# Attention and mixture of experts in one launch: weight loads a head ahead, packed probabilities, a ring of single rows for the gathers

## The chip, the cores and the metric

One core of a Trainium2 chip runs the whole program in one launch. The metric is the time of one execution on the device in microseconds (us), and the median of several executions is compared. Engines are named as in the profile: PE is TensorE, PEld its weight loads, DVE VectorE, ACT ScalarE, POOL GpSimd, SP SyncE. Line numbers (L83) are those of the kernel before.

## The reference, cut to what matters

```python
# B, S, D = 4, 512, 512;  H, HD = 16, 128;  E, K, I, SI = 16, 6, 352, 704
x = x + xattn(layernorm(x), ctx)             # softmax((ctx Wq' + bq)(ctx Wk' + bk)'), one head
hid = layernorm(x)
h = rmsnorm(hid, ln1_w)
q, k, v = h @ wq, h @ wk, h @ wv             # 16 heads of 128
scores = where(causal, q k' / sqrt(HD), -1e9)
hid = hid + (softmax(scores) v) @ wo
t = rmsnorm(hid, ln2_w)
probs = softmax(t @ gate_w.T); topv, topi = top_k(probs, 6); topv /= sum(topv)
routed = sum over the 6 chosen e: topv_e * ((silu(t eg_e') * (t eu_e')) @ ed_e')
shared = (silu(t sg') * (t su')) @ sd'
out = x + hid + routed + shared
```

Everything is float32. The kernel holds each float32 operand as a pair of float16 values (high part and remainder), and each product of the reference is three matmuls: high times high, high times remainder, remainder times high (`mm3`, L83, L86 and L87).

## The kernel before, in words

**Stages.** `xattn(b)` (a generator, one `yield` per piece) makes the first attention and the transposed input `hT[b]` of the second for each of four batches. Then comes a loop over 64 heads, which takes two batches at a time so that two neighbouring groups use the same weights (`path`, `heads`; a group `g` is two heads of one batch). After the heads come the shared feed-forward (`gate_up`, `shared_down`) of batches 0, 1 and 2, then 16 experts in order of their load, and the shared feed-forward of batch 3 as the last.

**One turn of the head loop (turn n).** `queries` computes the head's queries and keys (24 matmuls of 128x512, tiles `qk`, split into `qkt` by one ACT and one DVE instruction each). Every second turn `values` makes the values of both heads of the group. Then `project` (the output projection `wo` of a group that is complete), `scores(n)`, and `attend(n - LAG)` with LAG = 1. `scores` makes four blocks of rows (widths 128, 256, 384 and 512, since the mask is causal); each goes from PSUM through DVE (mask and maximum, L671), ACT (exp, L673), DVE (reciprocal, L675 and L676), ACT and DVE (`split` into float16 pairs, L73 and L74) into `pn`, and is then turned by a DMA transpose on SP's queue (`flip`, L91) into the tile `pt`. `attend` (tile `av`) multiplies `pt` by the values and splits the result into `ao`. So a head's `av` matmuls wait for the last of four transposes.

`pt` has 2 x 4 rows of 512: the transposed probabilities of key block k stand at rows 2k and 2k+1, and half of the rectangle is never written. `attend` runs over k, with one product of width 512, 384, 256 and 128 each: 4 x 3 = 12 matmuls and 3 x 1280 columns for each head.

**Weights.** The first use of each weight loads float32 into a staging tile, splits it, and writes the float16 pair to DRAM (L423, L429). The second pair of batches loads that pair (`fetch`, L414). All of these are DMAs on POOL's queue, issued in the turn that uses them, as far as the scheduler does not hoist them. The pools of `wqk`, `wv` and `wo` have two buffers each.

**Routing.** When a batch's last group is projected, `route1`, `route2` and `route3` normalize it, compute its gates (`lg`), rank the tokens within each expert (`rk`) and put 24 scatters of rows into a list. `scatter` issues a few of them in each turn (indirect DMAs on POOL, L467), and `pace` puts a one-element copy (`mark`, L457) that reads a recent result in front of them, so that they do not run ahead. In `route2` a running sum over the 16 experts takes four steps, each a DVE copy (L580) and a POOL addition (L581).

**Closing turns.** For n = 64 and 65 the first six pieces of `gate_up(0)` are mixed in, three in each turn.

**Gathers.** From the eleventh expert on, the expert results of each token are gathered from DRAM, one rank at a time: 16 indirect DMAs for each rank (`gather`, L1169 on POOL), each followed by an addition on DVE (L1178), which is pinned in program order. Their tiles hold three rows of 512 (2 buffers, six places), and the addition is issued when more than four gathers are outstanding.

**Order.** The program is written in this order, and a scheduler then moves instructions on each engine by the costs that it assumes; each engine runs its own list strictly in order. `after(a, b)` fixes an order of two instructions on one queue.

Of the kernel before, what the change touches and what calls it, by code (L numbers as in the profile page):

```python
# [9 lines left out]
F16 = mybir.dt.float16  # L10
# [7 lines left out]
P = 128  # L18
# [23 lines left out]
ON = 60  # L42
ROWS = E * T + 1
# [6 lines left out]
LAG = 1  # L50
# [5 lines left out]
def xattn_moe_block_kernel(ctx: ExitStack, tc: tile.TileContext, x, xT, ctxT, wqkx, bqk, ln1, ln2,  # L56
# [112 lines left out]
    ht = bpool("ht")  # L169
# [34 lines left out]
    def xattn(b):  # L204
# [37 lines left out]
        def wide(nm):  # L242
            return (ap_ if b else ht).tile([P, 2 * C, S], F16, tag=nm if b else "pt", name=f"{nm}{b}")
# [161 lines left out]
    held, partner, seen = {}, {}, set()  # L405

    def fetch(b, g, pool, tag, n, src, scr, nm):
        if held.get(nm, (None,))[0] == (b, g):
            return held.pop(nm)[1]
        w = pool.tile([P, 2, n], F16, tag=tag, name=f"{nm}_{b}")  # L410
        if (b, g) in partner:
            held[nm] = partner[b, g], w
        if nm in seen:
            nc.gpsimd.dma_start(w.rearrange("p a n -> p (a n)"), scr)  # L414
            return w
# [4 lines left out]
        else:  # L420
# [3 lines left out]
            if nm == "wqk1":  # L424
                after(ins, zz["hT", 0])
        for j, ins in enumerate(split(w[:, 0], w[:, 1], st_[:, :n], WS)):
            if first:
                after(ins, zz["nb"] if j else zz["calm"][0])
        ins = (nc.sync if nm == "wqk0" else nc.gpsimd).dma_start(scr, w.rearrange("p a n -> p (a n)"))  # L429
        if nm != "wqk0":  # L430
            zz["pad"] = ins
        if nm == "wqk0":
            after(ins, zz["ptp", 0])
        return w

# [20 lines left out]
    def pace(src):  # L456
        ins = nc.gpsimd.tensor_copy(mark, src)  # L457
        if "rrs" in zz:
            after(ins, zz["rrs"])
# [72 lines left out]
    def route2(b):  # L532
# [45 lines left out]
        for sft in (1, 2, 4, 8):  # L578
            nx = rp.tile([P, NT, E], F32, name="rcs", bufs=2)
            nc.vector.tensor_copy(nx[:, :, :sft], cs[:, :, :sft])  # L580
            nc.gpsimd.tensor_tensor(nx[:, :, sft:], cs[:, :, sft:], cs[:, :, :E - sft], ALU.add)  # L581
# [41 lines left out]
    def values(b, g):  # L623
        hb = hT[b]
        wvt = fetch(b, g, wg, "wv", C * GW, wv[g], wv_d[g], f"wv{g}").rearrange("p a (c d) -> p a c d", c=C)
# [11 lines left out]
    def queries(b, h):  # L637
        hb = hT[b]
        wt = fetch(b, h // HG, wp, "wqk", 1024, wqk[h], wqk_d[h], f"wqk{h}").rearrange("p l (a c d) -> p l a c d", a=2, c=C)
# [14 lines left out]
    def scores(b, h):  # L654
        qk = qks[b, h]
        pt = pts[b, h] = ht.tile([P, 2 * NT, S], F16, tag="pt", name="pt")
        for t in range(NT):
# [22 lines left out]
            flip(pt[:, :2 * (t + 1), tl], pn)  # L680

    def attend(b, h):
# [7 lines left out]
        for k in range(NT):  # L690
            mm3(pv[:, k * P:], [(vt[:, k, 0, hl], vt[:, k, 1, hl], pt[:, 2 * k, k * P:],
                                 pt[:, 2 * k + 1, k * P:])], start=k == 0, stop=k == NT - 1)
        split(ao[:, hh, 0], ao[:, hh, 1], pv, 1.0 / PS)

    def project(b, g):
# [4 lines left out]
        wot = fetch(b, g, wg, "wo", HG * D, wo[g], wo_d[g], f"wo{g}").rearrange("p a (c d) -> p a c d", c=HG)  # L700
# [15 lines left out]
    def gate_up(b, hid, tmp):  # L716
# [577 lines left out]
```

## Time and profile before

| what | value |
|---|---|
| median of 3 runs | 1769.27 us (1768.77 to 1786.13) |
| the profiled execution's own time | 1762.41 us |
| its span, first to last instruction | 1760.7 us |
| PE busy | 1708.6 us (97%), 9919 matmuls |
| DVE, ACT, POOL busy | 1116.2, 829.3, 485.1 us |
| mean granted TensorE clock | 0.993 |

A matmul's busy time reaches into the next one, since they are pipelined; the distance from one start to the next is what a matmul costs. The list of waits gives for each engine and line the idle time in front of it and what ended it, as a total, a count and the longest. Five columns matter in a timeline: start, duration, engine, line, and in brackets the idle time before it with its releaser.

### The profile page before, as it was taken

Reading aid. Unit: us, or ns where it says so; the run is one execution under the profiler, and the core shown is the slowest. Engines: PE = TensorE matmul, PEld = TensorE weight load, DVE = VectorE, ACT = ScalarE, POOL = GpSimd, SP = SyncE. Lnnn points to the kernel's source line nnn. Section 1 sums busy time; section 2 is a strip of 40 time slices with the busy share of each in tenths; the row PEclk is TensorE's granted clock in tenths of the full one; section 3 lists DMA queues with packets and bytes.
Section 4 is the critical chain, followed back from the end, with each engine's and each line's share of the span. In section 5 each row is a group of like instructions: output and inputs, shape, how many; then the busy total and the mean of one; then the engine's idle time right before and its main releaser. Section 6 shows DMA issues by size and latency. Waiting matters only on the chain. (4 is left out here: it accounts for less than half of the span.)

```text
span 1760.7 us, 27659 instructions
## 1 busy us (share of the span) xinstructions
PE 1708.6 (97%) x9919; PEld 932.9 (53%) x9919; DVE 1116.2 (63%) x2766; ACT 829.3 (47%) x1711; POOL 485.1 (28%) x614
## 2 busy tenths in 40 slices
PE   7899999999998999999999999999999999999998
PEld 3555556565654555556555544455555555555553
DVE  6787877787785676776667647544434344356755
ACT  4565655565643545454445422344544445444431
POOL 5524212240255242121113454300000000034654
PEclk9999999999999999999999999999999999999999
DMA  7787867575687787556547653755554546589866
GB/s 246 181 205 184 225 150 192 122 196 118 138 183 187 163 177 179 120 120 118 111 104 132 140 155 128 247 173 148 150 173 137 154 143 163 154 228 254 221 198 213
DMA packets 392212, 296.24 MB, mean 168 GB/s; under 512 B 334880, under 2 KB 335136, under 8 KB 391296
## 3 DMA queue, kind: packets, MB, share of 16 engines
q1 hardware_dynamic: 353360, 159.87, 39.9%
q0 software_dynamic: 38704, 134.51, 25.5%
q8 instruction: 80, 1.31, 0.3%
q14 instruction: 68, 0.56, 0.1%
HBM read 124.81 MB, written 88.94 MB: 121 GB/s over the span
## 5 line engine op out<-in xcount | busy, mean ns | idle before, releaser
L1169 POOL DMA_INDIRECT yg<-y_d,yrc x96 | 109.9, 1145 | 505.2 <-PE u L87 426.0
L673 ACT ACTIVATE pe<-pe,bnm 128x128 f32<-128x128 f32 (+3 forms) x256 | 142.5, 557 | 161.5 <-DVE bnm L671 161.3
L83 PE MATMUL qk<-hT,wqk 128*128 128x512 f16 (+1 forms) x520 | 196.4, 378 | 9.1 <-DMA wqk<-wqk_d 5.5
L86 PE MATMUL qk<-hT,wqk 128*128 128x512 f16 (+1 forms) x520 | 196.5, 378 | 0.0
L87 PE MATMUL qk<-hT,wqk 128*128 128x512 f16 (+1 forms) x520 | 196.3, 377 | 0.0
L74 DVE SCALAR_TENSOR_TENSOR pn<-pe,brc,pn 128x128 f16<-128x128 f32 (+3 forms) x256 | 148.1, 590 | 21.3 <-ACT pn L73 18.0
L671 DVE CUSTOM_DVE_ANT_0 pe<-sc,causal 128x128 f32<-128x128 f32 (+3 forms) x256 | 117.0, 485 | 66.9 <-PE sc L668 65.9
L73 ACT ACTIVATE pn<-pe,brc 128x128 f16<-128x128 f32 (+3 forms) x256 | 133.5, 553 | 34.1 <-ACT pe L673 17.8
L83 PE MATMUL v<-wv,hT 128*128 128x256 f16 x512 | 139.8, 273 | 0.9 <-DMA hT<-hh 0.9
L87 PE MATMUL v<-wv,hT 128*128 128x256 f16 x512 | 139.7, 273 | 0.0
L86 PE MATMUL v<-wv,hT 128*128 128x256 f16 x512 | 139.7, 273 | 0.0
L83 PE MATMUL g<-xT,wt 128*128 128x384 f16 (+2 forms) x384 | 127.3, 331 | 0.0
L86 PE MATMUL g<-xT,wt 128*128 128x384 f16 (+2 forms) x384 | 127.2, 331 | 0.0
L87 PE MATMUL g<-xT,wt 128*128 128x384 f16 (+2 forms) x384 | 127.2, 331 | 0.0
L1058 ACT ACTIVATE hT_e<-hf 128x384 f16<-128x384 f32 (+3 forms) x96 | 51.1, 532 | 133.6 <-DVE hf L1072 133.2
L83 PE MATMUL y<-dt,hT_e 128*128 128x512 f16 (+1 forms) x288 | 109.4, 380 | 0.0
L87 PE MATMUL y<-dt,hT_e 128*128 128x512 f16 (+1 forms) x288 | 108.9, 378 | 0.0
L86 PE MATMUL y<-dt,hT_e 128*128 128x512 f16 (+1 forms) x288 | 108.9, 378 | 0.0
L73 ACT ACTIVATE qkt<-qk 128x512 f16<-128x512 f32 x128 | 75.1, 587 | 70.7 <-PE qk L87 70.5
L705 DVE SCALAR_TENSOR_TENSOR x<-wo,x 128x512 f32<-128x512 f32 x128 | 87.2, 685 | 33.3 <-PE wo L87 32.9
L467 POOL DMA_INDIRECT xs_d<-h2p,slotu x96 | 98.7, 1028 | 28.3 <-issue 27.1
L74 DVE SCALAR_TENSOR_TENSOR qkt<-qk,qkt 128x512 f16<-128x512 f32 x128 | 87.5, 684 | 18.3 <-ACT qkt L73 15.2
(333 smaller groups left out, 4041.5 us busy)
## 6 DMA issues: line engine op xcount, KB each, us to landing
y_d<-yt SPq DMA_DIRECT2D x96, 256.0 KB, 2.8
est<-in_ew_dram SPq DMA_DIRECT2D x32, 704.0 KB, 6.2
est<-in_ed_dram SPq DMA_DIRECT2D x16, 768.0 KB, 4.7
wqk<-wqk_d POOLq DMA_DIRECT2D x20, 512.0 KB, 5.0
wqk_d<-wqk POOLq DMA_DIRECT2D x15, 512.0 KB, 4.0
wqk_st<-in_wqk_dram POOLq DMA_DIRECT2D x14, 512.0 KB, 6.4
xs_d<-causal POOLq DMA_DIRECT2D x16, 384.0 KB, 5.6
wv<-wv_d POOLq DMA_DIRECT2D x10, 512.0 KB, 5.7
```

The lines of the kernel that those rows point to most:

```text
L73: return (nc.scalar.activation(hi, src, AF.Copy, scale=scale), nc.vector.scalar_tensor_tensor(lo, src, scale, hi, ALU.mult, ALU.subtract))
L74: nc.vector.scalar_tensor_tensor(lo, src, scale, hi, ALU.mult, ALU.subtract))
L83: ins = nc.tensor.matmul(o, lh, rh, start=start and j == 0, stop=False)
L86: nc.tensor.matmul(o, lh, rl, start=False, stop=False)
L87: ins = nc.tensor.matmul(o, ll, rh, start=False, stop=stop and j == n - 1)
L467: ins = nc.gpsimd.indirect_dma_start(out=xs_d, out_offset=bass.IndirectOffsetOnAxis(ap=slotu[:, tt, k:k + 1], axis=0), in_=h2ps[tt], in_of ...
L671: nc.vector.tensor_tensor_reduce(pe, ps[:, :w], causal[:, S - w:], -1.0, 3e38, ALU.add, ALU.min, nm)
L673: nc.scalar.activation(pe, pe, AF.Exp, bias=nm, scale=-1.0, accum_out=sm)
L705: nc.vector.scalar_tensor_tensor(x2[:, t, :], ps, 1.0 / (VS * WS), x2[:, t, :], ALU.mult, ALU.add)
L1058: nc.scalar.activation(hT[:R, ic, :w], hf, AF.Copy)
L1169: nc.gpsimd.indirect_dma_start(out=yg, out_offset=None, in_=src, in_offset=bass.IndirectOffsetOnAxis(ap=idx[:, tt, k:k + 1], axis=0))
```

## The change

1. `LAG` is 2: `attend` runs two turns behind `scores`. The pool of `pt` has three buffers (`LAG + 1`).
2. `pt` is packed: row block t of the scores fills rows t(t+1) to (t+1)(t+2) of a tile of 20 x 128, without the empty half. `attend` takes row blocks in pairs, so that each product covers at most 256 columns: 6 x 3 = 18 matmuls for each head, the same 3 x 1280 columns.
3. `wqk` and `wv` are fetched one turn ahead (`early=True`, second use only), `wo` right after the `attend` that completes a group. `pace` now also stands behind the latest load. The write of the split weights to DRAM (`save`) is put off until the next load has been issued.
4. The running sum's additions in `route2` go from POOL to DVE.
5. The closing turns: turn 64 has two pieces of `gate_up(0)`, then `attend` of both last heads, then a third piece; turn 65 has the other three. The hidden tiles of `gate_up(0)` take two pieces each instead of three.
6. Gathers use a ring of 7 tiles of one row each, with 5 outstanding; the hidden tiles of the shared feed-forward get a pool of their own, and for the last batch the experts' staging tiles.
7. In the first turns, `xattn(1)` advances by 0 pieces in turn 0 and by 3 in turns 1 to 5, instead of 2 in each.

```diff
+RING = 7
-LAG = 1
+LAG = 2
...
-    ht = bpool("ht")
+    ht = bpool("ht", LAG + 1)
...
-    def fetch(b, g, pool, tag, n, src, scr, nm):
+    def fetch(b, g, pool, tag, n, src, scr, nm, early=False):
+        if early and nm not in seen or soon.get(nm) and early:
+            return
         if held.get(nm, (None,))[0] == (b, g):
-            return held.pop(nm)[1]
-        w = pool.tile([P, 2, n], F16, tag=tag, name=f"{nm}_{b}")
+            return None if early else held.pop(nm)[1]
+        w = soon.pop(nm, None)
+        if w is None:
+            w = pool.tile([P, 2, n], F16, tag=tag, name=f"{nm}_{b}")
+            if nm in seen:
+                zz["load"] = nc.gpsimd.dma_start(w.rearrange("p a n -> p (a n)"), scr)
+        if early:
+            soon[nm] = w
+            return
...
-        ins = (nc.sync if nm == "wqk0" else nc.gpsimd).dma_start(scr, w.rearrange("p a n -> p (a n)"))
...
+        else:
+            unsaved.append((scr, w))
+    def save(keep, behind=None):
+        while len(unsaved) > keep:
+            scr, w = unsaved.pop(0)
+            zz["pad"] = nc.gpsimd.dma_start(scr, w.rearrange("p a n -> p (a n)"))
+            if behind:
+                after(zz["pad"], behind)
...
     def pace(src):
         ins = nc.gpsimd.tensor_copy(mark, src)
-        if "rrs" in zz:
-            after(ins, zz["rrs"])
+        for k in ("rrs", "load"):
+            if k in zz:
+                after(ins, zz[k])
...
-            nc.gpsimd.tensor_tensor(nx[:, :, sft:], cs[:, :, sft:], cs[:, :, :E - sft], ALU.add)
+            nc.vector.tensor_tensor(nx[:, :, sft:], cs[:, :, sft:], cs[:, :, :E - sft], ALU.add)
...
-        pt = pts[b, h] = ht.tile([P, 2 * NT, S], F16, tag="pt", name="pt")
+        pt = pts[b, h] = ht.tile([P, NT * (NT + 1), P], F16, tag="pt", name="pt")
-            flip(pt[:, :2 * (t + 1), tl], pn)
+            flip(pt[:, t * (t + 1):(t + 1) * (t + 2), :], pn)
...
-        for k in range(NT):
-            mm3(pv[:, k * P:], [(vt[:, k, 0, hl], vt[:, k, 1, hl], pt[:, 2 * k, k * P:],
-                                 pt[:, 2 * k + 1, k * P:])], start=k == 0, stop=k == NT - 1)
+        for t in range(0, NT, 2):
+            for k in range(t + 2):
+                q = max(k, t)
+                o = pv[:, q * P:(t + 2) * P].rearrange("p (n q) -> p n q", q=P)
+                first = q * (q + 1) + 2 * k
+                phi, plo = (pt[:, first + a:first + a + 2 * (t + 1 - q) * (q + 1) + 1:2 * (q + 1), :] for a in range(2))
+                mm3(o, [(vt[:, k, 0, hl], vt[:, k, 1, hl], phi, plo)], start=k == 0, stop=k == t + 1)
...
-    for n in range(NH + LAG + 1):
+    for n in range(NH + 2):
...
+            if n + 1 < NH:
+                b, h = heads[n + 1]
+                wqk_of(b, h, True)
+                if h % HG == 0:
+                    wv_of(b, h // HG, True)
...
-            for ic in range(3 * (n - NH), 3 * (n - NH) + 3):
...
+            hs0 = chunks(*((3, 6) if n > NH else (0, 2)))
...
-        if 0 <= m < NH:
-            b, h = heads[m]
+        for i in [m] * (0 <= m < NH - LAG) + [NH - 2, NH - 1] * (n == NH):
+            b, h = heads[i]
             attend(b, h)
             if h % HG == HG - 1:
                 ready.append((b, h // HG))
+                wo_of(b, h // HG, True)
+        if n == NH:
+            chunks(2, 3)
...
-            step(1, 2)
+            step(1, 3 * (n > 0))
...
-    lookahead(lambda: st2.tile([P, 3, D], F32, tag="hs", name="yg"), 3, 4)
+    hctx.close()
+    ring_p = ctx.enter_context(tc.tile_pool(name="ring", bufs=RING, side="right", reuse_waits="tile"))
+    lookahead(lambda: ring_p.tile([P, 1, D], F32, name="yg"), 1, RING - 2)
...
-    gather_all(0)
+    gather_all()
```

The scheduler's order of both kernels can be read off the built programs. TensorE has 384 matmuls and 384 weight loads more (64 heads x 6). ACT has two loads of a function table more, both in the closing turns. POOL has 17 instructions less, DVE 16 more; SP's count is unchanged.

## The prediction

> **What bounds the kernel now.** I read the page first (busy shares), then the waits of TensorE, then timelines of the places that they name.
>
> ```profile
> span 1760.7 us, 27659 instructions
> ...
> PEclk9999999999999999999999999999999999999999
> ```
>
> ```profile
> PE av L83 <- DMA pt<-pn: 16.9, 10, 3.9
> PE xm L83 <- DMA ptp<-pn: 9.8, 2, 5.8
> PE qk L83 <- DMA wqk<-wqk_d: 5.5, 1, 5.5
> PE u L1081 <- DVE hf L1072: 3.9, 2, 2.1
> PE qk L83 <- DMA hT<-hh: 3.6, 2, 3.2
> PE sc L667 <- DVE brc L676: 0.3, 1, 0.3
> ```
>
> TensorE is busy for 97% and its idle time is a short list: all eleven of its waits sum to 44 us. So the matmuls set the time, and a change can only take these waits away, add new ones, or change the matmuls. What a matmul costs is the step from one start to the next, not the duration shown:
>
> ```profile
> 701.90 0.27 PE L83 MATMUL av<-pt,vt 128*128 128x256 f16 x1
> 702.01 0.27 PE L86 MATMUL av<-pt,vt 128*128 128x256 f16 x1
> 702.12 0.27 PE L87 MATMUL av<-pt,vt 128*128 128x256 f16 x1
> 702.23 0.22 PE L83 MATMUL av<-pt,vt 128*128 128x128 f16 x1
> 702.28 0.22 PE L86 MATMUL av<-pt,vt 128*128 128x128 f16 x1
> 702.34 0.33 PE L666 MATMUL sc<-qkt,qkt 128*128 128x384 f16 x1
> ```
>
> 256 columns take 0.11 us and 128 take 0.055; from the same timeline, 512 take 0.215 and 384 take 0.162. That is 0.417 ns a column and 2.3 ns a matmul. With these steps all recorded matmuls sum to 1687 us; the other 64 us up to the last matmul's start are the 44 us of waits and some 20 us in which the steps are longer. Part of that is a halved clock after a wait:
>
> ```profile
> 300.00:325.00 25.00, 25.00 (x141) 13.15 (x139) 20.63 (x56) 13.25 (x31) 3.45 (x5) 1.00 0.57 127
> 540.00:555.00 15.00, 9.49 (x51) 5.27 (x50) 4.43 (x15) 2.78 (x9) 7.15 (x9) 0.77 0.95 211
> 965.00:980.00 15.00, 11.09 (x131) 8.58 (x130) 8.24 (x35) 4.47 (x10) 4.11 (x8) 0.89 0.87 155
> ```
>
> The third number from the end is the granted clock: 1.00 in the quiet stretch, 0.77 around the wait for `wqk`, 0.89 around the longest wait for `pt`. 0.11 of 15 us is 1.7 us; 0.23 of 15 is 3.4 us, of which 2.6 us fall after the wait, on running matmuls.
>
> **The change, part by part.** Distances below are "matmul time": the matmuls standing between two instructions in TensorE's order, each at its step above.
>
> *A. Values two turns behind.* In the old order the distance from a head's last scores to its `av` has a median of 15.6 us and a least of 9.1; 27 of 64 heads have under 14. The heads that waited needed their distance plus their wait: 11.2 us (9.4 + 1.7, the wait at 513 us), 13.9 (11.2 + 2.6, at 585 us), 19.1 (15.0 + 4.0, at 970 us, behind four transposes of `route1`), 19.2 for one at 193 us. The new order gives a median of 24.0 and a least of 12.1, and one head under 14; for those ten heads it is 17.7 to 27.4, enough for nine, 0.6 us short for the one at 193 us. Removed: 16.9 + 1.7 of clock - 0.6 = 18.0 us. The third buffer of `pt` keeps SP's queue as free as it was: a transpose of head n needs the product of head n-3, where it needed that of n-2 with two buffers. What is late next after a wait for `pt` was only `ao` and `wo`, which follow.
>
> *B. Loads ahead.*
>
> ```profile
> 539.89 0.60 POOL L414 DMA_DIRECT2D wqk<-wqk_d  x1
> ...
> 548.81 0.61 PE L83 MATMUL qk<-hT,wqk 128*128 128x512 f16 x1 [5.51 <-DMA wqk<-wqk_d]
> ```
>
> This load stood behind ten scatters of 1.3 us each and landed 8.9 us after its issue. In the new order on POOL it stands before the whole burst. Removed: 5.5 + 2.6 of clock = 8.1 us. But the next load (head 4 of batch 2) now stands behind 20 scatters: from the last `rk` 7 us to the first scatter, 20 x 1.28 = 25.6, about 4 for what lies between them, 0.6 issue and 8.9 landing are 46 us, and the matmuls up to its use are 46.2 us. No margin: between 0 and 4 us, I take 1, since the DMA queues are emptier by then. Net -7.0 us. The loads of `wv` and `wo` never held TensorE. The writes to DRAM that wait for a split (41.3 us on `wqk_d`, with the next load queued behind them) go behind that load; nothing reads them for hundreds of us. `mark`, and with it the scatters, stands behind the latest load: if that load waits for its buffer, they wait with it, but only the experts read them.
>
> *C. First turns.* `xm` of batch 1 waits 4.0 us at 76.6 us. The new order puts only six score matmuls (3 x 0.11 + 3 x 0.215 = 1.0 us) in front of it; what it waits for is unchanged. -1.0 us; at best the short clock loss behind it goes too (-2.5), at worst 0.
>
> *D. Ring of gathers.*
>
> ```profile
> 1623.47 0.75 DVE L1178 SCALAR_TENSOR_TENSOR acc<-yg,cws,acc 128x512 f32<-128x512 f32 x1 [1.95 <-DMA yg<-y_d,yrc]
> 1624.14 1.75 DVE L74 SCALAR_TENSOR_TENSOR dt<-est,dt 128x1536 f16<-128x1536 f32 x1
> 1625.81 0.55 DVE L1072 SCALAR_TENSOR_TENSOR hf<-u,sg 128x384 f32<-128x384 f32 x1
> ```
>
> An addition waits on DVE for its gather, `hf` stands behind it and TensorE behind `hf`, twice, 3.9 us in all. An addition now comes after five later gathers instead of four: 5 x 1.27 = 6.4 us of issues against a usual landing of 4.7, where 5.1 left almost nothing. -3.0 us (0 to -3.9).
>
> *E. 18 products for 12.* The columns stay the same, so by the row above 384 x 2.3 ns = +0.9 us. Here the Trainium skill speaks against the change: "TensorE: Matmul & The Clock Gate", section "Back-to-back issue gap", says that in a real stream of weight loads and matmuls a 128-column matmul sustains only about 81 ns, since both operations count. Then each of the 384 would cost 81 - 53 = 28 ns (53 being 128 columns at 0.417 ns), +10.6 us. The trace has exactly this form, three 128-column products after a wider one with a new weight load each, at 55 ns, and the new order has them in threes as well: I take 0.9. The moving operand now has a step between its two blocks, which no row shows; bounds 0 and, if each 256-column product cost as two of 128, 64 x 12 x 2.3 ns = 1.8 us. Taken: 0.
>
> *F. What A moves together.* Moving `av` and `wo` away shortens another distance: from the last `qk` to the head's first scores it was under 4 us for 2 heads, now for 19 (3.4 to 3.8, before mostly 4.7). ACT (0.59) and DVE (0.69) split each of two tiles, about 1.8 us in the usual case. Measured from the end of that split to the first score, nine of 64 heads had under 1.1 us left, three nothing. If all 64 lost 1.1 us, that would be 5.4 us; 19 of 64 is +1.5 us (0 to 5).
>
> *G. Closing turns.* Two more table loads of 1.28 us on ACT lie between the last head's exponentials; the distance to its `av` is 20.0 us where 16.7 were enough. From the last `wo` to `lg3` it falls from 19.4 to 14.9, and the normalization, split and transposes in between took about 13.5. +1 us (0 to 4).
>
> *H.* The running sum: 16 POOL additions of 0.27 to 0.29 us become DVE ones; DVE is busy for 63% and gates are not waited for: 0. The hidden tiles' new places: 0, their buffers are long free.
>
> Sum: -18.0 - 7.0 - 1.0 - 3.0 + 0.9 + 1.5 + 1.0 = -25.6 us. The span would be 1760.7 - 25.6 = 1735.1. The profiled execution took 1762.4 us and the median is 1769.3; I subtract from the median: **1743.7 us**. With every bound at its best end (-18.6 - 8.1 - 2.5 - 3.9 + 0.9) it is 1737.
>
> **Rivals.**
>
> *Half given back.* The gain of A and B is there, but the load behind 20 scatters comes 4 us late and the clock halves (2 more), F costs 5, G 4 with a clock loss of 2, D saves nothing: against the sum +5, +3.5, +5, +3: 1760 us. For it: each of these distances is at its edge. Against: they would all have to go wrong.
>
> *The waits go, the time doesn't (the change doesn't do what it says).* If the wait for `pt` were due to SP's queue and not to the distance, it would move with `av`. Then only C, D and half of B remain, -1 - 3 - 4, and +3.4 for E, F, G: 1765. For it: one landing of 10.4 us at 960 us. Against: the ten waits fell on heads with short distances, or behind `route1`.
>
> *Slower.* F decides: `qkt` of the 19 short heads. At a latency of 3.6 us from `qk` to a finished `qkt` it costs nothing, at 3.6 + 25.6/19 = 4.9 it eats the gain, and at 5.9 the kernel is 1% slower, 1788 us. For it: six of 64 heads did take over 4 us. Against: the median is 1.8 us, and DVE and ACT have idle time in each turn.
>
> **How the numbers follow.** The sum as stated 0.68 (its own range 1737 to 1750), half given back 0.15, no change 0.08, slower 0.09. A measurement of this kernel can tell about 1% from no change: faster is under 1751.6. Half of "half given back" would still fall under it: 0.68 + 0.08 = 0.76 faster, 0.07 + 0.08 = 0.15 same, 0.09 slower. Below 1735 the bounds leave nothing; above, the range goes to 1762, which holds the sum and "half given back" and leaves out the rest.
>
> **What would show it.** A: no wait for `pt` in TensorE's list but a short one near 190 us. B: no wait for `wqk`, clock 1.00 around it. C: still 3 us at 75 us. D: the waits of `u` for `hf` under 1 us. E: 128-column products of `av` 0.055 us apart; at 0.08 the skill's rule was right. F: a new row, `sc` waiting for `qkt`; over 20 us there would make the prediction wrong. G: no wait at `lg` and `sy`.

## The result and the profile after

| | before | after |
|---|---|---|
| median of 22 runs each | 1769.19 us | 1781.78 us |
| ratio, 95% interval | | 1.0080 (1.0057 to 1.0102) |
| profiled execution, its span | 1762.41, 1760.7 us | 1774.29, 1772.2 us |
| PE busy, matmuls | 1708.6 us, 9919 | 1718.3 us, 10303 |
| waits of TensorE, all | 44 us | 46.6 us |
| mean granted clock | 0.993 | 0.989 |

After is 0.8% slower. The prediction was 1743.7 us, 1.4% faster, and its range ended at 1762 us. The page of after:

```profile
span 1772.2 us, 28420 instructions
...
PEclk9999999999999999999999999999999999999999
```

The clock row, in tenths, hides what the windows below show. TensorE's list of waits is still short. The same view as for before (total, count, longest):

```profile
PE sc L695 <- DVE bnm L700: 9.4, 6, 2.8
PE qk L84 <- DMA hT<-hh: 6.5, 2, 3.3
PE xm L84 <- DMA ptp<-pn: 6.4, 1, 6.4
PE lg L569 <- DMA h2T<-h2p: 3.8, 2, 2.5
PE sc L695 <- ACT pm L317: 2.9, 1, 2.9
PE av L84 <- DVE ao L75: 2.0, 1, 2.0
PE sc L695 <- ACT qkt L74: 1.8, 1, 1.8
...
PE su L87 <- issue: 1.6, 2, 0.8
...
PE av L84 <- DMA pt<-pn: 0.7, 1, 0.7
```

The waits that the change was to remove are gone: `pt` 16.9 to 0.7 us, `wqk` and `u` for `hf` off the list. What stands there now is of the same size. New at the top are scores (`sc`) that wait for `bnm`, the maximum that DVE (L700) takes of an earlier block of scores. In this program TensorE does not write a score block into a bank of PSUM (its result memory) before DVE has read what stands there. A head has four blocks and the scores have three banks, so that blocks 0 and 2 share one (in both kernels, `t` is the number of the block):

```python
            if t == 2:
                ps = low
            else:
                ps = bank("s", f"sc{b}_{h}_{t}")
            if t == 0:
                low, ps = ps[:, P:], ps[:, :P]
```

Block 2 (384 wide) thus waits for the maximum of block 0 of its own head, and the next head's first blocks wait for those of this head. These waits for `bnm` are not on the list of before, and no step of the prediction has them.

The clock, too, is lower at other places. The windows of after (the third number from the end is the granted clock):

```profile
300.00:325.00 25.00, 25.00 (x152) 13.86 (x150) 18.78 (x51) 11.78 (x27) 3.93 (x6) 1.00 0.58 153
540.00:555.00 15.00, 14.78 (x97) 8.68 (x96) 13.56 (x44) 8.04 (x22) 7.75 (x14) 1.00 0.85 166
176.00:187.00 11.00, 6.23 (x36) 3.29 (x34) 7.75 (x18) 6.93 (x15) 3.76 (x4) 0.80 1.16 284
655.00:665.00 10.00, 7.83 (x57) 5.54 (x55) 5.05 (x24) 4.16 (x13) 3.81 (x9) 0.83 0.57 170
965.00:980.00 15.00, 12.11 (x64) 6.42 (x63) 10.28 (x25) 5.57 (x15) 6.38 (x8) 0.89 0.78 183
...
1060.00:1072.00 12.00, 8.20 (x86) 4.21 (x85) 7.63 (x19) 2.78 (x5) 6.30 (x8) 0.77 0.86 195
```

The place of the `wqk` wait now has the full clock, as step B said. But three new places are at 0.77 to 0.83, where before had the full clock:

```profile
176.00:187.00 11.00, 10.75 (x78) 7.40 (x77) 10.14 (x30) 9.37 (x22) 4.34 (x7) 1.00 0.66 221
655.00:665.00 10.00, 10.00 (x63) 5.65 (x61) 7.17 (x25) 5.33 (x14) 6.91 (x10) 1.00 1.00 227
1060.00:1072.00 12.00, 12.00 (x69) 5.55 (x66) 7.77 (x35) 5.24 (x8) 2.74 (x10) 1.00 0.01 2
```

Over the whole span, (1 - 0.993) x 1760.7 = 12.3 us of full clock were missing before and (1 - 0.989) x 1772.2 = 19.5 us after. The 2.6 us more of waits and the 7.2 us more of missing clock make 9.8 of the 11.5 us by which the span grew. This is a rough account: the clock is given to 0.001, which is 1.8 us of the span, and clock that is missing during a wait costs nothing.

To place losses, I use one number below: the loss of a stretch, the sum of the distances from one matmul's start to the next, less what the matmuls cost (0.417 ns a column and 2.3 ns each; 25 ns for one of 16 columns, as measured). One profile is one execution, and executions of one kernel differ by 20 us and more, so the ratios judge and the losses only tell where to look. The two profiled executions are each about 7 us under their kernel's median.

| loss in us, by stretch of time | 0-100 | 100-200 | 200-500 | 500-700 | 700-950 | 950-1100 | 1100-1600 | 1600-1700 | over 1700 |
|---|---|---|---|---|---|---|---|---|---|
| before | 23.1 | 4.4 | 1.2 | 17.0 | 2.6 | 7.1 | 3.1 | 4.4 | 0.8 |
| after | 22.5 | 11.4 | 4.9 | 8.6 | 1.2 | 16.3 | 3.8 | 0.2 | 6.9 |

The gain is at 500 to 700 us and at the gathers (1600 to 1700). It is given back at 100 to 500, in the closing turns and in the last stage.

### The profile page after: what moved, and what is told of

Same layout as the page of the kernel before. It is cut to its first block, busy times and chain, and to the rows that moved or that the text cites. A ratio compares the mean times of both kernels' runs of the same rounds, so it can differ in the third digit from the quotient of the medians.

```text
span 1772.2 us, 28420 instructions
## 1 busy us (share of the span) xinstructions
PE 1718.3 (97%) x10303; PEld 964.8 (54%) x10303; DVE 1124.3 (63%) x2782; ACT 831.5 (47%) x1713; POOL 489.5 (28%) x597
## 4 chain that ended last, share of the span: by engine, by line
PE 55%; DVE 2%; DMA 2%; issue 1%; POOL 1%; ACT 0%; another core or an unknown queue 0%; SPq 0%; DVEq 0%; ACTq 0%; POOLq 0%
PE g L87 4%; PE g L84 4%; PE g L88 4%; PE y L84 4%; PE y L87 4%; PE y L88 4%; PE u L88 2%; PE u L84 2%; PE u L87 2%; PE qk L84 2%; PE qk L87 2%; PE qk L88 2%; PE u L1137 1%; PE u L1138 1%; PE wo L88 1%; PE wo L84 1%
## 5 line engine op out<-in xcount | busy, mean ns | idle before, releaser
L1225 POOL DMA_INDIRECT yg<-y_d,yrc x96 | 119.1, 1241 | 497.6 <-DMA y_d<-yt 429.4
L700 DVE CUSTOM_DVE_ANT_0 pe<-sc,causal 128x128 f32<-128x128 f32 (+3 forms) x256 | 114.9, 484 | 10.0 <-PE sc L697 9.9
```

Source lines behind the costliest of these rows:

```text
L700: nc.vector.tensor_tensor_reduce(pe, ps[:, :w], causal[:, S - w:], -1.0, 3e38, ALU.add, ALU.min, nm)
L1225: nc.gpsimd.indirect_dma_start(out=yg, out_offset=None, in_=src, in_offset=bass.IndirectOffsetOnAxis(ap=idx[:, tt, k:k + 1], axis=0))
```

## Experiments: one part alone

Ratios are against the kernel before on the same chip. A diff is against the kernel that its heading names.

**Values two turns behind alone** (before, with parts 1, 2 and 5).

```diff
-LAG = 1
+LAG = 2
...
-    ht = bpool("ht")
+    ht = bpool("ht", LAG + 1)
...
+        for i in [m] * (0 <= m < NH - LAG) + [NH - 2, NH - 1] * (n == NH):
...
```

> The kernel before with parts 1, 2 and 5 alone: values two turns behind, packed pt with three buffers, the closing turns and hidden tiles of the change; loads, saves, gathers, running sum and first turns as before. Theory N (new waits): the waits of av for pt go (-17 us) but scores wait for their PSUM banks and the closing turns for lg, together 15 to 20 us, so the time is within 4 us of before. Rival M (the 384 extra matmuls are dear): no bank waits to speak of, but 128-column products of av at 0.07 us or more, +5 to +10 us of longer steps. Rival L (the loss comes from the other parts: loads, saves, first turns, gathers): this kernel is 12 to 18 us faster than before, as step A had it.

Measured: 1776.5 us, 1.0054 (1.0033 to 1.0075). The profiled execution lost 64.7 us in all, as before (63.8); but it is the fastest of the 22, 14 us under their median, so it shows which waits there are and not what the median lost. TensorE's waits in it, in part:

```profile
PE sc L667 <- DVE bnm L672: 4.9, 3, 1.9
...
PE av L83 <- DVE x L710: 4.0, 2, 3.6
PE wo L83 <- DVE x L710: 3.4, 3, 1.5
PE sc L667 <- ACT qkt L73: 3.3, 2, 1.8
```

Neither `pt` nor `wqk` is on the list, though the loads are issued as before. The scatters, which held up the `wqk` load, now come a turn later, since the routing does, and the load is issued ahead of them:

```profile
528.11 0.54 POOL L415 DMA_DIRECT2D wqk<-wqk_d  x1
...
542.82 1.13 POOL L468 DMA_INDIRECT xs_d<-h2p,slotu  x1 [0.17 <-issue]
```

So what step B gave to the early loads comes here from the order alone; and with both gains in hand this kernel is slower by 0.5%. Rival L (12 to 18 us faster) falls. Theory N was nearest but had the time within 4 us of before, and 15 to 20 us of waits for banks and `lg`; this profile has 4.9 and 1.3.

**The packed rows and 18 products alone** (before).

```diff
-            flip(pt[:, :2 * (t + 1), tl], pn)
+            flip(pt[:, t * (t + 1):(t + 1) * (t + 2), :], pn)
...
-        for k in range(NT):
+        for t in range(0, NT, 2):
+            for k in range(t + 2):
...
```

> The kernel before with the packed rows of pt and the 18 products alone (two buffers, one turn behind). Step E said +0.9 us; theory N: +1 us, within 3 us of before, steps of 0.055 us for 128 columns. Rival M: +8 to +11 us, steps of 0.08 us.

Measured: 1793.05 us over six executions, 1.0126 (1.0085 to 1.0168): slower than theory N and rival M had it. But products of 128 columns stay 0.055 us apart, as in after itself:

```profile
705.30 0.22 PE L84 MATMUL av<-pt,vt 128*128 128x128 f16 x1
705.35 0.22 PE L87 MATMUL av<-pt,vt 128*128 128x128 f16 x1
705.41 0.22 PE L88 MATMUL av<-pt,vt 128*128 128x128 f16 x1
705.47 0.27 PE L84 MATMUL av<-pt,vt 128*128 128x256 f16 x1
```

So the products are cheap, and the cost is a wait. In the packed kernel:

```profile
PE av L83 <- DMA pt<-pn: 28.2, 16, 4.2
```

Fourteen of these sixteen waits are in the middle of a head's products, at the seventh, where the second pair of row blocks begins. The first pair needs only two of the four transposes; the scheduler saw its data ready sooner and put the products earlier (median distance from the last scores 14.6 us of matmul time, 15.6 before), where the second pair's transposes had not landed. The waits for `pt` are 11.3 us more than before; the mean clock of this profile is 0.986 over 1785.9 us, so 25.0 us of full clock were missing, 12.7 more than before. Together that is 24.0 of the 25.2 us by which this span is longer.

**The same with the pairs in falling order.**

```diff
-        for t in range(0, NT, 2):
+        for t in (2, 0):
```

> The packed rows and 18 products alone again, but with the pair of row blocks 2 and 3 first and the pair 0 and 1 second. Packing with the pairs in rising order cost 1.3%, with 128-column products still 0.055 us apart; its waits for pt rose from 16.9 to 28.2 us, ten of sixteen of them in the middle of a head's products, since the first pair needs only two transposes and the scheduler put it earlier. With the pairs reversed the first product needs all four transposes, and the distance from a head's last scores to its first product is as in before (median 16.0 us). Theory O (order): within 3 us of before, waits for pt 14 to 20 us. Rival M (the packed form itself is dear, in the products, in the transposes or in the strided operand): still 1% or more slower.

Measured: 1764.97 us, 0.9995 (0.9972 to 1.0018), and

```profile
PE av L83 <- DMA pt<-pn: 11.2, 8, 3.8
```

Theory O holds, with fewer waits than its 14 to 20 us, and rival M falls. One reversed loop is worth 1.3% here (1.0126 against 0.9995).

**Loads ahead alone** (before).

```diff
+            if n + 1 < NH:
+                b, h = heads[n + 1]
+                wqk_of(b, h, True)
...
```

> The kernel before with the loads of wqk, wv and wo ahead alone; the writes to DRAM stay where they were. Step B: the wait for wqk at 548 us goes with its halved clock, -7 us. Theory N: B's gain is real, -5 to -8 us. Rival W (the ahead loads only move the wait to the next load behind 20 scatters): 0 to -3 us and a new wait for wqk near 600 us.

Measured: 1768.43 us, 0.9992 (0.9968 to 1.0016). The wait stays:

```profile
540.81 0.60 POOL L425 DMA_DIRECT2D wqk<-wqk_d  x1
...
552.25 0.61 PE L83 MATMUL qk<-hT,wqk 128*128 128x512 f16 x1 [8.03 <-DMA wqk<-wqk_d]
```

Asked for one turn ahead, the load is still behind the same ten scatters (540.81 us; 539.89 before). It lands 11 us after issue. Both theories had expected some gain.

**Ring of gathers alone** (before; part 6 of the change).

> The kernel before with the ring of seven single rows for the gathers alone, and the new places of the hidden tiles. Step D: -3 us, the waits of u for hf under 1 us. The profile of after shows five stalls of instruction issue in the last shared feed-forward, 1734 to 1739 us, 4 us in all with a halved clock after them. Theory N1: they come with the ring and stand in this profile too, so the sum is 0 to +3 us. Rival N2: they are an accident of one execution or come from another part; then -3 to -4 us.

Measured: 1769.14 us, 1.0013 (0.9992 to 1.0034). `u` for `hf` is 1.8 us (3.9 before); 7.3 us are lost after 1700 us. The time is within N1's bounds, and the -3 us of step D is not there.

## Experiments: one part undone

Each heading says what the kernel after is changed by, unless the text names another kernel.

**Four banks for scores.**

> The kernel after with four PSUM banks for scores and two for queries, values and gates (three and three before). Theory N (the scores wait for a bank that DVE L700 still has to read): the 9.4 us of sc waiting for bnm go to under 2 us; part may come back as qk or v waiting for their own banks; the time is 0 to 8 us under after. Rival Q (the wait is DVE's backlog, whatever the banks): the same 8 to 10 us appear in front of other matmuls, and the time is that of after.

```diff
-    NB = dict(a=3, s=3, w=2)
+    NB = dict(a=2, s=4, w=2)
```

1793.59 us over six executions, 1.016 (1.0116 to 1.0205). Scores no longer wait for `bnm` to speak of, but `rk` does for POOL (9.3 us), queries for `qkt` (3.8), `xq` for `vt` (3.3), and `av` for `pt` again (7.8). It doesn't separate the theories: a bank taken elsewhere costs more, and the order changed too. Nor does a fourth bank part blocks 0 and 2 of a head, which still share one; a bank of its own for block 2 was not tried.

**Three pieces first in the closing turns.**

> The kernel after with all three first pieces of the shared feed-forward ahead of the last two heads' products in turn 64 (part 5 undone in its order). Between 950 and 1100 us after loses 16 us over its matmul steps where before loses 7. Theory N (the closing turns' order costs it): that falls to 8 to 11, the waits for lg under 2 us, time 5 us under after. Rival (the loss there comes from values two turns behind, whatever the order of the pieces): 14 to 18 us again.

```diff
-            hs0 = chunks(*((3, 6) if n > NH else (0, 2)))
+            hs0 = chunks(*((3, 6) if n > NH else (0, 3)))
...
-        if n == NH:
-            chunks(2, 3)
```

1778.72 us, 1.0085 (1.0049 to 1.0121); 13.3 us lost between 950 and 1100. That lies between theory (8 to 11) and rival (14 to 18), nearer to the rival: the order of the pieces is not the main cause.

**Two pieces of batch 1 in each first turn.**

> The kernel after with part 7 undone: two pieces of batch 1's first attention in each of turns 0 to 5. Theory N: the wait for batch 1's hT at 143 us (3.3 us) and the score waits at 182 to 186 us (5 us, with a halved clock of 3.4) are due to part 7, so the loss of 11.4 us between 100 and 200 us falls to about 4, and the wait for ptp at 76 us is 4 us instead of none; time 5 us under after. Rival: the waits at 182 to 186 come from the late xT load on POOL's queue and stay; then only 2 to 3 us.

```diff
-            step(1, 3 * (n > 0))
+            step(1, 2)
```

1778.88 us, 1.0065 (1.0043 to 1.0086); the loss at 100 to 200 us is 6.3 (11.4 in after), but batch 1's `hT` is as late (3.4 us) and `xm` waits 5.1 us again. Part 7 costs little or nothing that the ratios can tell. The score waits near 182 us are gone here, but back in the mended kernel below with the same two pieces. In after they begin with ACT, which stands for a load of `xT`, and DVE behind ACT:

```profile
176.78 1.06 ACT L273 ACTIVATE lnp<-xT 128x1024 f16<-128x1024 f32 x1 [5.76 <-DMA xT<-in_xT_dram]
178.16 2.03 DVE L75 SCALAR_TENSOR_TENSOR pn<-pe,brc,pn 128x128 f16<-128x128 f32 x1 [6.76 <-ACT pn L74]
```

**Loads and saves as before.**

> The kernel after with part 3 undone: each weight is loaded in the turn that uses it and written to DRAM at once, and the copy in front of the scatters no longer stands behind the loads. The same part alone on before gained nothing, and values two turns behind alone already had no wait for wqk near 550 us. Theory N (part 3 gains nothing once the scatters come a turn later, and its bunched writes make xT late at 177 us): no wait for wqk over 1 us, the score waits at 182 to 186 us shrink, time 0 to 5 us under after. Rival B (step B as predicted): a wait for wqk of 5 us or more with its halved clock, time 5 to 8 us over after.

```diff
-            if n + 1 < NH:
-                b, h = heads[n + 1]
-                wqk_of(b, h, True)
...
+            save(0)
```

1774.27 us, 1.0059 (1.0033 to 1.0086). No wait for `wqk`, and none of scores near 182 us: theory N. Part 3 is worth nothing that these ratios can tell in either order.

**Gathers without the ring**, measured twice, the second time on one chip with after itself (which has no edit).

```diff
-    lookahead(lambda: ring_p.tile([P, 1, D], F32, name="yg"), 1, RING - 2)
+    lookahead(lambda: st2.tile([P, 3, D], F32, tag="hs", name="yg"), 3, 4)
```

> The kernel after without the ring of gathers (part 6 undone, the hidden tiles' places too). With the ring the loss at the gathers between 1600 and 1700 us is 0.2 us in all of after's family (4.4 before), but after 1700 us it is 6.7 to 8.6 us in all of them (0.8 before), with TensorE itself stalled on instruction issue at sg and su. Theory N1 (the ring brings both): 3 to 8 us at 1600 to 1700, under 3 us after 1700, no issue stalls of TensorE, time 0 to 4 us under after. Rival N2 (the last stage stalls at random, other kernels without the ring lost 4.7 and 7.9 us there): 5 to 8 us after 1700 again, time 0 to 4 us over after.

> The kernel after, unchanged, a second time, beside the three others. The first time it was 0.8% slower than before, and one profile of it had the stalls of instruction issue in the last stage. Theory N1 (the ring of gathers brings them): again 5 us or more lost over the matmul steps after 1700 us, and 1.006 to 1.010 of before. Rival N2 (an accident of one execution): under 2 us there.

> The kernel after without the ring a second time, now beside after itself. The first time it came out 0.16% slower than before, with the other losses of after unchanged in its profile. Theory N1: under 2 us lost after 1700 us again, 8 to 12 us faster than after by the medians. Rival N2: within 4 us of after.

The first: 1765.33 us, 1.0016 (0.9992 to 1.0041). On one chip, after again: 1779.27 us, 1.0051 (1.0019 to 1.0082), and without the ring again: 1772.69 us, 1.0040 (1.0007 to 1.0074). By these ratios the kernel without it is the faster both times, by 0.6% (against after's ratio on another chip) and by 0.1%; the second difference is inside its interval. The loss after 1700 us was 0.8 and 4.2 us without the ring, 6.9 and 6.1 with it. But a kernel with the ring (the one without early loads) lost 0.8 there, and one without it lost 7.6, with the same stalls of TensorE (the two-turn kernel of the last pair below):

```profile
1725.68 0.38 PE L84 MATMUL sg<-h2T,shw 128*128 128x512 f16 x1 [1.04 <-issue]
...
1727.81 0.38 PE L84 MATMUL sg<-h2T,shw 128*128 128x512 f16 x1 [1.03 <-issue]
```

So the ring doesn't make these stalls, N1 falls as to their cause, and what does make them stays open. In the second run of after, `u` waited 4.5 us for `hf` with the ring.

**Back to one turn behind for the last heads.** This one is an edit of the first kernel of the section above (values two turns behind alone), with the pairs in falling order as well.

> The kernel before with parts 1 and 2 alone (values two turns behind, packed pt, pairs of row blocks in falling order), but back to one turn behind for the last three heads, so that the closing turns are those of before. The same with the change's closing turns was 0.5% slower than before: over its matmul steps it lost 14.3 us between 950 and 1100 us where before loses 7.1, and nothing for pt elsewhere. Theory N (values two turns behind gain 10 us in the head loop, and its end gives it back): 6 to 9 us between 950 and 1100, and 5 to 9 us faster than before. Rival (being two turns behind costs as much in bank and DVE waits inside the loop, wherever it ends): 12 to 15 us there or elsewhere, and within 3 us of before or slower.

```diff
-            hs0 = chunks(*((3, 6) if n > NH else (0, 2)))
+            hs0 = chunks(*((3, 6) if n > NH else (0, 3)))
...
-        for i in [m] * (0 <= m < NH - LAG) + [NH - 2, NH - 1] * (n == NH):
+        for i in [m] * (0 <= m < NH - 4) + {NH - 2: [NH - 4, NH - 3], NH - 1: [NH - 2], NH: [NH - 1]}.get(n, []):
```

1766.58 us, 1.0028 (0.9999 to 1.0057). The loss in the closing turns is 7.1 us, as before (14.3 with the change's closing turns), so that part of theory N held. But no gain appears, as its rival said: the profile loses about 7 us less than before at 500 to 700 us and about 8 us more at 100 to 500. The kernel with the same pairs one turn behind was 0.9995.

**Several parts undone at once** (called the mended kernel): in after, the closing turns of the kernel just above, and the edits above for the gathers, the first turns and the pairs' order, together.

> The kernel after with parts 5, 6 and 7 undone (closing turns as before with the last three heads one turn behind, gathers without the ring, two pieces of batch 1's attention per turn) and the pairs in falling order; values two turns behind, the packed pt, loads ahead and the running sum on DVE stay. Theory N: the losses of after at 140 to 190 us, at 950 to 1100 and after 1700 us go, 8 to 15 us under after and 0 to 6 us faster than before. Rival (parts 1 and 2 themselves cost it): still 0.4% or more slower than before.

1767.68 us, 1.0032 (1.0006 to 1.0059); scores waited 17.0 us for `bnm` in its profile, one of its slowest executions (1777.39 us). Theory N (no slower than before) falls, and the rival's 0.4% is not quite reached. Undoing the ring alone gave 1.0016 on the same chip, so undoing the rest as well shows no gain.

**No scatters while a batch is routed**: before, packed in falling pairs.

> A candidate to beat both: the kernel before with the packed pt (pairs in falling order) and no scatters in the two turns in which a batch is routed, so that the load of wqk near 550 us stands behind one scatter instead of ten. The falling pairs alone were 0.05% faster than before, with a wait for wqk of 2.1 us and a halved clock. Theory: no wait for wqk over 0.5 us, 4 to 8 us faster than before. Rival: the scatters bunch in the turns after and delay another load, within 2 us of before.

```diff
-        if scat and n < NH:
+        if scat and n < NH and n not in agenda:
```

1772.19 us, 1.0034 (1.0001 to 1.0067). No wait for `wqk`, but 23.2 us for `pt` (7.1 at 589 us). TensorE now waits for the transposes instead; why was not followed.

## What the score waits are made of

Ahead of the long score waits that I followed, DVE had not been busy but standing. The clearest is in the second profile of after (start, duration, engine, and in brackets the idle time with what ended it):

```profile
661.50 1.25 POOL L558 TENSOR_TENSOR x1t<-x1t,x 128x512 f32<-128x512 f32 x1 [11.24 <-DMA x1t<-x_d]
...
664.68 0.32 POOL L612 TENSOR_TENSOR rcs<-rcs,mf 128x64 f32<-128x64 f32 x1
665.03 0.43 DVE L636 TENSOR_TENSOR oh<-rcs,kp 128x96 f32<-128x96 f32 x2 [10.35 <-POOL rcs L612]
665.37 0.28 DVE L700 CUSTOM_DVE_ANT_0 pe<-sc,causal 128x128 f32<-128x128 f32 x1
...
665.72 0.48 PE L695 MATMUL sc<-qkt,qkt 128*128 128x384 f16 x1 [8.28 <-DVE bnm L700]
```

Read it upwards. TensorE stood 8.28 us for a maximum of 0.28 us on DVE. DVE stood 10.35 us for a product of 0.32 us on POOL. POOL stood 11.24 us for the load of a residual that nothing near needs. Each engine runs its list strictly in order, so that one late load stopped four of them (ACT stood 11.79 us for the same maximum). In before, POOL stood 6.67 us for such a load, but the scheduler had put other work in front on DVE, which then stood 2.10 us for `rcs`.

The matmul that waits is block 2 of a head and the maximum that of block 0: the two that share a bank. POOL is not always the one behind the wait by this product. In after itself the wait of 2.13 us at 659 us is of this kind; the longest, 2.77 us at 973 us, came after DVE had stood for another product of POOL,

```profile
968.88 0.75 DVE L529 SCALAR_TENSOR_TENSOR h<-x,rrs,ln2b 128x512 f32<-128x512 f32 x1 [4.47 <-POOL h2p L79]
```

and those near 76 and 182 us after DVE had stood 4.09 and 6.76 us for ACT.

Two turns behind, there is less room for this. From 100 to 1070 us DVE waited for scores 65.9 us before and 9.9 us after:

```profile
DVE pe L671 <- PE sc L668: 65.9, 48, 8.5
```

```profile
DVE pe L700 <- PE sc L697: 9.9, 18, 1.5
```

Before, DVE was usually early for the scores, and a stall of DVE came out of that slack; after, the scores are usually there first. DVE's waits for POOL in the same stretch grew from 19 to 36 us.

**Taking the partner away** (after without the ring):

```diff
-        nc.gpsimd.tensor_tensor(cs, cs, mf, ALU.mult)
-        nc.gpsimd.tensor_tensor(pr, pr, rv.unsqueeze(2).to_broadcast([P, NT, E]), ALU.mult)
+        nc.vector.tensor_tensor(cs, cs, mf, ALU.mult)
+        nc.vector.tensor_tensor(pr, pr, rv.unsqueeze(2).to_broadcast([P, NT, E]), ALU.mult)
```

> The kernel after without the ring and with two more of the routing's small multiplications on DVE in place of POOL (the running sum times the mask, and the gates times their reciprocal). In profiles with values two turns behind, DVE stands idle for 4 to 9 us in front of `oh` until POOL has made `rcs`; the scores' maximum is queued behind it on DVE, and TensorE waits 2 to 5 us for a PSUM bank, near 660 us in six of six kernels. Theory D (in-order DVE behind a slow partner is what makes the score waits): the wait near 660 us goes, 2 to 4 us under the kernel without the ring. Rival (the banks are short whatever DVE waits for): the wait stays.

1771.26 us, 1.0033 (0.9995 to 1.0071). The score waits without and with this edit, on the same chip:

```profile
PE sc L695 <- DVE bnm L700: 10.5, 3, 5.3
```

```profile
PE sc L695 <- DVE bnm L700: 1.6, 4, 0.8
```

The longest of the first list is

```profile
665.06 0.48 PE L695 MATMUL sc<-qkt,qkt 128*128 128x384 f16 x1 [5.30 <-DVE bnm L700]
```

behind 8.02 us in which DVE stood for `rcs`. With two small products moved off POOL it is gone, with the banks as they were: theory D holds for this wait, by one profile of each. The other two, 2.8 us at 78 us and 2.4 us at 185 us, stand before the first `rcs` (at 537 us), so that what they lost in the second list is no effect of this edit. In the median it is 1.4 us, too little to tell.

**Taking the whole cause away**, two turns and one turn behind: the additions and products of the running sum all on DVE, and the residual's addition one turn after its load. The first is against the mended kernel, the second against the packed one in falling pairs.

```diff
-            nc.gpsimd.tensor_tensor(x1t, x1t, x2[:, t, :], ALU.add)
-            nc.gpsimd.dma_start(r_d[b][:, t, :], x1t)
+            came.append((b, t, x2, x1t))
...
+        for b, t, x2, x1t in [came.pop(0)] if came else []:
+            ins = nc.gpsimd.tensor_tensor(x1t, x1t, x2[:, t, :], ALU.add)
```

> Two turns behind, with the cause of the score waits taken away as far as it is known: the mended kernel (parts 5, 6 and 7 undone, falling pairs), the routing's running sum, mask and gate multiplications all on DVE, and the residual's addition on POOL put one turn after its load, where POOL stood 4 to 11 us for that load with `rcs` queued behind it. Theory D: the 17 us of sc waiting for bnm in the mended kernel fall under 5, the wait of 5 us at 1014 us goes, 8 to 14 us under the mended kernel (1.0032 of before), so 2 to 8 us faster than before. Rival (the waits wander on to the next side work that DVE stands behind): 10 us or more of score waits at other places, still not faster than before.

> The same two mendings of the side work, but with values one turn behind as in before (packed pt in falling pairs; loads, gathers and closing turns of before). If being two turns behind is worth something once DVE isn't held up, this kernel is 5 us or more slower than the other of this pair, with its 11 to 17 us of waits for pt. Theory D by itself also expects a gain here, 2 to 6 us under before, since POOL's standing for the residual holds up DVE in this order too (19 us of DVE waiting for POOL in the profile of before, 36 us in after).

Two turns behind: 1762.97 us, 0.9983 (0.9959 to 1.0007); one turn behind: 1770.73 us, 1.0026 (0.9994 to 1.0058). In the first, scores wait

```profile
PE sc L699 <- DVE bnm L704: 3.2, 2, 1.8
```

where the mended kernel had 17.0, of which 12.7 us were at the three places behind POOL (548, 668 and 1014 us). Theory D holds for the waits. In time, this kernel is 0.5% under the mended one and has the lowest ratio of all kernels here, but its interval still holds 1. One turn behind, the same edits gained nothing (1.0026, and 0.9995 without them), although theory D expected 2 to 6 us there too. So freeing DVE seems to pay where the values are two turns behind, and only there. That is suggested and not shown: the ratios come from three chips, the last two intervals overlap, and the two kernels differ in the loads and saves as well, which were worth nothing alone.

## Why the prediction was wrong, by its steps

**A failed.** The waits for `pt` went from 16.9 to 0.7 us, so the distances were read rightly. The step that failed is the sentence on what is late next: "What is late next after a wait for `pt` was only `ao` and `wo`, which follow." The next thing late was the scores of a following head, behind their banks and DVE: 9.4 + 2.9 us in after, and 5.1 us of full clock missing behind them (3.4 at 182 us, 1.7 at 660 us). That is 17.4 us where step A had -18.0. The ratios say the same: parts 1, 2 and 5 alone measured 1.0054 where -18 us would be 0.990, and two turns behind with the closing turns of before 1.0028, one turn behind 0.9995. Alone, the ring (1.0013) and the loads (0.9992) add little, so most of after's loss (1.0080, the second time 1.0051) comes with parts 1, 2 and 5. How much of it is the score waits in the loop and how much the closing turns is not settled. The slower rival (1788 us) was nearest in its number. It named the scores, but `qkt` in front of them, where the banks and DVE behind them weighed more. The rival "the waits go, the time doesn't" had the outline, but by SP's queue, and the waits for `pt` did not move along.

**B: right effect, wrong cause.** The wait for `wqk` and its halved clock are gone, but by the later routing of A. The early loads alone left a wait of 8.0 us; undoing them brought none back. The feared next load was not late.

**C**: the 4.0 us of `xm` turned into 2.4 us of scores at 75.6 us with the clock halved as before. The stretch to 100 us lost 0.6 us less. Not counted at all was the other side: batch 1's `hT`, 3.3 us late at 143 us.

**D**: `u` had no wait for `hf` in one profile of after and 4.5 us in the other; alone, the ring was 1.0013. The -3.0 does not show.

**E right**, against the 81 ns that it takes from the Trainium skill ("TensorE: Matmul & The Clock Gate", section "Back-to-back issue gap"): 128 columns cost 0.055 us in after, and 18 products cost nothing that can be measured (0.9995). What was missed is that the packing's loop order also moves the products in the schedule, worth 1.3% with one turn behind. Two turns behind there is room for it: after has the rising order and 0.7 us of waits for `pt`.

**F** inside its bounds: waits for `qkt` are 1.8 + 0.8 + 0.8 = 3.4 us (1.5 predicted, 0 to 5), and far from deciding.

**G** mis-sized: the closing turns lose 16.3 us (7.1 before), +9 where +1 and at most 4 stood. `lg` waits 3.8 us, `wo` for DVE 1.6 us, and the clock halves at 1066 us. The end of the two-turn order has more to do with it (7.1 us with the end of before) than the order of the pieces (13.3), by one profile each. The mended kernel has the end of before too, and lost 13.7 us there; its score waits at 983 and 1014 us make 6.6 of them.

**H**: no wait of TensorE in after belongs to the additions. But one multiplication left on POOL kept DVE waiting for the same queue.

The clock has its part. The Trainium skill ("TensorE: Matmul & The Clock Gate", section "HAM oscillation — how this bites in real kernels") gives as the rule to avoid idle gaps over about 3.4 us. By it, none of after's score waits would have cost clock. The traces show otherwise. In after the clock halved behind a score wait of 2.13 us (657.31 to 659.44 us):

```profile
656.99:660.40 3.41, 1.24 (x14) 0.69 (x13) 1.55 (x10) 0.79 (x3) 1.64 (x5) 1.00 0.67 154
660.40:663.82 3.42, 3.42 (x20) 2.35 (x17) 2.78 (x9) 2.19 (x8) 0.44 (x2) 0.50 0.68 249
```

In the packed kernel in falling pairs it stayed full around a wait of 3.77 us for `pt` (582.18 to 585.95 us):

```profile
580.68:584.09 3.41, 1.50 (x7) 0.49 (x5) 2.29 (x9) 1.71 (x6) 1.59 (x3) 1.00 1.18 274
584.09:587.50 3.41, 1.55 (x14) 1.30 (x15) 0.00 (x0) 0.00 (x0) 0.00 (x0) 1.00 1.08 332
587.50:590.92 3.42, 3.42 (x23) 1.81 (x21) 2.63 (x10) 2.63 (x7) 0.00 (x0) 1.00 0.30 45
```

The windows are not chosen freely. Within each of the twenty traces, all halvings start on one grid of 3.41 us, and these are its steps. That fits the window of about 3.4 us that the same page (section "What's actually happening") says runs free. The first wait lies in one step, so that TensorE was busy for 1.24 of 3.41 us; the second is cut in two, with 1.9 us idle in each. I counted the steps of all twenty traces from 30 us on that had the full clock. When TensorE was idle for more than 2.0 us of a step, the clock was half in the next one, 107 times of 107. Between 1.7 and 2.0 us it was 10 times of 36, and below 1.7 us never in over 9800 steps. A halving lasts one step or more, and one step at half the clock is 1.7 us of full clock. So the prediction's clock terms were in part a matter of luck: a wait between 2 and 4 us halves the clock or not by where the grid cuts it, and the grid lies elsewhere in each execution.

## What to carry to other kernels

A list of waits names what was last, not what is scarce: before moving work away from a wait, ask which instruction is queued next behind the same in-order engine, and which buffer or bank it needs. When an engine waits, follow it upwards until an engine waits for something no one needs yet; here a 0.3 us product behind a residual's load on POOL stopped DVE, and moving it took away a score wait of 5 us, though too little of the time to measure. When a loop order changes what is needed first, look where the scheduler puts it: one reversed loop was 1.3%. And before counting a wait's gain in full, ask what else the same engines are late with.

## What the runs showed that was not expected

In the last stage TensorE, ACT and DVE stood for several us with no releaser that the trace knows ("issue", "remote") in some of the kernels: up to 8.6 us are lost after 1700 us, with and without the ring, and 0.8 in others. No part of the change was found to make it, and its cause is open. The one profile of before had none of it, so the prediction could not see it there.
